# Product 2 of the third layer on the second Strassen level, its relation in three PE steps, and an order of issue with preferences of its own for that layer

## The chip, the core and the metric

The kernel runs on one core of a Trainium2 chip. The metric is device time in microseconds for one execution of the whole program, median of three runs. Profiles are of one execution each; the engines are called PE (matrix products), DVE, ACT and POOL (elementwise work) and SP (which issues most DMAs). One matmul in fp32 leaves two records in the trace.

## The reference

Four layers work on x of 128 graphs x 64 nodes x 512 features. Each normalises, applies relu, and adds a layer of attention over the graph's nodes to x. The third layer is the one that the change is about:

```python
h = jnp.maximum(_layernorm(x, axis=-1), 0.0)
x = x + _L2_gnn_ref(h, adj, L2_gnn_Wq, L2_gnn_Wk, L2_gnn_Wv)

def _L2_gnn_ref(neuron_states, adjacency, Wq, Wk, Wv):
    ...
    q = jnp.einsum('bnd,ed->bne', neuron_states, Wq)
    k = jnp.einsum('bnd,ed->bne', neuron_states, Wk)
    v = jnp.einsum('bnd,ed->bne', neuron_states, Wv)
    rel = jnp.einsum('bnd,bmd->bnm', q, k)
    rel = adjacency.T[None, :, :] * rel
    rel = rel / jnp.linalg.norm(rel, axis=2, keepdims=True)
    return jnp.einsum('bnm,bmd->bnd', rel, v)
```

The other three are attention with a softmax in 8 heads; the second and the fourth have an output projection, and the fourth a second normalisation behind it.

## The kernel before, in words

**Tiles.** The 8192 rows of x are cut into 16 tiles of 512 rows, and the main loop runs over n = 0 to 63: four layers of 16 tiles. Tile n is prepared (`layer_norm`, line 810) while tile n-1 is in its products. Its normalised rows are turned: ACT splits them into halves of words (`z`), SP issues a transposing DMA (`hp<-z`), and ACT copies `hp` into `hT` (`turn`, line 799). POOL then forms sums of quarters of hT (`sums_x`, line 855, tiles S and S2).

**Products on two levels.** Each projection of 512x512 by 512x512 is a Strassen product in Winograd's form: 7 products (1 to 7) of 256x256 by 256x256 instead of 8. One such product is 4 matmuls of 256 moving columns (`prod_T`, `prod_N`). A product may again be split into 7, of 128x128 by 128x128: then it is 7 matmuls of 128 columns (`prod_2`, line 905). The table LEVEL2 says which products of which projection are split: 4, 2 and 3 in most, but only 4 and 3 in `a2` and `v2`, the two projections of the third layer (`a2` has Wq and Wk folded into one matrix). Its sums of weights are made once (`sums_q_w`, line 705), its sums of x for each tile (`sums_q`, line 874). ORDERS (line 920 on) gives the order of the products in a projection: the digits in quotes are split, "a", "b" and "c" are the parts that the split products have in common, and each opens or shares a PSUM bank (HOME). ACT copies the first result of a quarter out of PSUM, DVE adds the later ones, POOL adds some pieces in SBUF (`projection`, line 928).

**The relation** of the third layer (`relate`, line 1331) is one step of PE for two tiles: for the tile before, the squares' sums (`ones` by `sq`) and rel by v into four banks; for the present tile, hT by gT into a fifth. DVE and ACT then make rel and its squares, POOL the reciprocal norms, and DVE scales the products of rel and v and adds them to xo, which SP stores. xo has one buffer, so its next load comes behind the store.

**The order of issue** is not that of the code. Every instruction is recorded as a step with its engine, a cost and its dependences (class Plan, line 57), and `order` (line 170) lists all of them engine by engine before anything is issued: of the steps that are ready on an engine it takes the earliest, and of those that with the smallest rank. The rank is a due time counted back from PE's sequence, plus an entry of the table PREFER for the step's kind (`kind`, line 160: engine, operation, tiles, size), less HASTE for steps that read PSUM. A PE step that opens a bank waits until one is free by that account, and may be at most WINDOW openings ahead. Accumulating DMAs of POOL (`add_out`, line 1292) add whole tiles to x in DRAM. All instructions are issued at line 313, which is why most profile lines name it.

Of the kernel before, what the change touches and what calls it, by code (L numbers as in the profile page):

```python
# [19 lines left out]
P = 128  # L20
G = 64
D = 512
# [34 lines left out]
class Plan:  # L57
# [4 lines left out]
    def __init__(self, nc):  # L62
        self.nc = nc
        self.steps, self.products, self.lags, self.front = [], [], {}, set()
        self.wrote, self.readers, self.known = {}, {}, {}
        self.group = None
        self.hot = set()
        for e in ("tensor", "vector", "scalar", "gpsimd", "sync"):
            setattr(self, e, Engine(self, e))
# [48 lines left out]
    def add(self, eng, calls, reads, writes, busy, late):  # L118
# [16 lines left out]
        self.steps.append([eng, calls, deps, busy, late])  # L135

# [23 lines left out]
    def kind(self, i):  # L160

        eng, calls = self.steps[i][:2]
        op, a, k = calls[0]
        aps = [v for v in list(a) + list(k.values()) if isinstance(v, bass.AP)]
        tags = [re.sub(r"(_\d+)+$", "", v.tensor.name) for v in aps]
        ins = [t for t in tags[1:] if t != "ident"][:1]
        name = f"{eng[:3]} {op} {tags[0]}<-{''.join(ins)}"
        return name if eng == "sync" or "x1" in name else f"{name} {aps[0].free_size()}"
# [170 lines left out]
class Pool:  # L339
# [34 lines left out]
ROOM = 5  # L374
ON_DVE = ""
WINDOW = 6
RESERVE = 0
HASTE = 17721.0
# [5 lines left out]
    "gps dma_start out_0_dram<-xo 2048": 5763,  # L384
    "gps dma_start x1<-kT": -946,
    "gps dma_start x1<-row": 14864,
    "gps memset mhalf<- 8": 5987,
    "gps memset ones<- 1": -3681,
    "gps tensor_scalar nb<-mv 4": -2896,
    "gps tensor_scalar ve<-mv 4": -6369,  # L390
    "gps tensor_tensor S2<-S 128": 9,
    "gps tensor_tensor S2<-S2 128": 741,
    "gps tensor_tensor S2<-hT 128": 632,
    "gps tensor_tensor S<-S 128": -41337,
    "gps tensor_tensor S<-S 512": -723,
    "gps tensor_tensor S<-hT 512": -6132,
    "gps tensor_tensor SO2<-SO 128": 396,
    "gps tensor_tensor SO2<-oT 128": -23951,
    "gps tensor_tensor SO<-SO 128": -50741,
    "gps tensor_tensor SO<-SO 512": 9602,  # L400
    "gps tensor_tensor SO<-oT 512": -33296,
    "gps tensor_tensor hT<-hT 128": -4880,
    "gps tensor_tensor kT<-kT 128": -5077,
    "gps tensor_tensor kT<-kT 256": 2384,
    "gps tensor_tensor kT<-kT 512": 11213,
    "gps tensor_tensor nb<-nb 1": -15986,
    "gps tensor_tensor nb<-nb 4": -3108,
    "gps tensor_tensor oT<-oT 128": -4027,
    "gps tensor_tensor qT<-qT 128": 12457,
    "gps tensor_tensor qT<-qT 256": -1197,  # L410
    "gps tensor_tensor rn<-ss 8": -6949,
    "gps tensor_tensor row<-hT 128": 11559,
    "gps tensor_tensor row<-row 128": -12998,
    "gps tensor_tensor rs<-ve 1": 813,
    "gps tensor_tensor rs<-ve 4": 10508,
    "gps tensor_tensor s<-hT 128": -31894,
    "gps tensor_tensor s<-s 1024": -44252,
    "gps tensor_tensor s<-s 128": 2292,
    "gps tensor_tensor v<-v 128": -5381,
    "gps tensor_tensor v<-v 256": -116,  # L420
    "gps tensor_tensor w<-w 128": 27797,
    "gps tensor_tensor w<-w 256": 34174,
    "gps tensor_tensor w<-w 512": 19861,
    "gps tensor_tensor xo<-xo 128": -2823,
    "gps tensor_tensor xo<-xo 256": 11906,
    "gps tensor_tensor xo<-xo 512": -26610,
    "sca activation kT<-mm 128": -14518,
    "sca activation kT<-mm 256": -7008,
    "sca activation qT<-mm 128": -14547,
    "sca activation qT<-mm 256": 1806,  # L430
    "sca activation s<-s 1024": 228608,
    "sca activation s<-s 256": 22995,
    "sca activation xin<-xin 512": 14211,
    "sca copy hT<-hp 1024": -86946,
    "sca copy hT<-mm 512": 16570,
    "sca copy kT<-mm 128": -51749,
    "sca copy kT<-mm 256": -10379,
    "sca copy kT<-mm 512": 312,
    "sca copy oT<-mm 512": 2819,
    "sca copy p5<-mm 128": -15649,  # L440
    "sca copy qT<-mm 128": -2476,
    "sca copy qT<-mm 256": -51590,
    "sca copy qT<-mm 512": -10049,
    "sca copy s<-hp 1024": 2630,
    "sca copy s<-mm 512": -22036,
    "sca copy v<-mm 128": -984,
    "sca copy v<-mm 256": 13038,
    "sca copy v<-mm 512": 40409,
    "sca copy w<-mm 128": 218,
    "sca copy w<-mm 256": 121,  # L450
    "sca copy xo<-mm 128": -10549,
    "sca copy xo<-mm 256": -34241,
    "sca copy xo<-mm 512": 7433,
    "sca copy z<-hp 1024": 3064,
    "sca copy z<-mm 512": -3311,
    "sca copy z<-oT 1024": -50937,
    "sca copy z<-s 1024": -9197,
    "sca copy z<-xin 1024": 18596,
    "syn dma_start a2d<-z": -1267,
    "syn dma_start adj2<-in_adj_dram": 25859,  # L460
    "syn dma_start bk1<-in_L1_gnn_bk_dram": 15719,
    "syn dma_start bq0<-in_L0_gnn_bq_dram": 5813,
    "syn dma_start bq1<-in_L1_gnn_bq_dram": -1214,
    "syn dma_start oT<-in_L2_gnn_Wq_dram": 3993,
    "syn dma_start oT<-in_L2_gnn_Wv_dram": 21834,
    "syn dma_start out_0_dram<-qT": -4023,
    "syn dma_start out_0_dram<-xo": -5129,
    "syn dma_start qT<-out_0_dram": -7867,
    "syn dma_start row<-in_L0_gnn_bv_dram": 12123,
    "syn dma_start row<-in_L3_gnn_b_proj_dram": -11681,  # L470
    "syn dma_start row<-in_L3_gnn_ln_beta_dram": -563,
    "syn dma_start row<-in_L3_gnn_ln_gamma_dram": 188,
    "syn dma_start v2d<-z": -4221,
    "syn dma_start w<-a2d": 3351,
    "syn dma_start w<-in_L0_gnn_Wk_dram": -18017,
    "syn dma_start w<-in_L0_gnn_Wq_dram": 6737,
    "syn dma_start w<-in_L0_gnn_Wv_dram": 12382,
    "syn dma_start w<-in_L1_gnn_Wk_dram": -32703,
    "syn dma_start w<-in_L1_gnn_Wo_dram": 24621,
    "syn dma_start w<-in_L1_gnn_Wq_dram": -15904,  # L480
    "syn dma_start w<-in_L1_gnn_Wv_dram": -8884,
    "syn dma_start w<-in_L3_gnn_w_proj_dram": 13379,
    "syn dma_start w<-in_L3_gnn_w_qkv_dram": -1695,
    "syn dma_start w<-v2d": -8508,
    "syn dma_start x1<-xo": -647,
    "syn dma_start xin<-in_x_dram": -8353,
    "syn dma_start xin<-x1": -13444,
    "syn dma_start xo<-in_x_dram": 31957,
    "syn dma_start xo<-x1": 15761,
    "ten matmul mm<-S 128": 4706,  # L490
    "ten matmul mm<-S 256": 5870,
    "ten matmul mm<-SO 128": -29146,
    "ten matmul mm<-SO 256": 3875,
    "ten matmul mm<-hT 128": 7283,
    "ten matmul mm<-hT 256": -141,
    "ten matmul mm<-hT 64": -4249,
    "ten matmul mm<-oT 128": -1749,
    "ten matmul mm<-oT 256": -7085,
    "ten matmul mm<-qT 64": 9858,
    "ten matmul mm<-row 128": -14789,  # L500
    "ten matmul mm<-s 1": -12970,
    "ten matmul mm<-s 128": 4783,
    "ten matmul mm<-s 64": -16805,
    "ten matmul mm<-w 128": -1692,
    "ten transpose mm<- 128": 4281,
    "ten transpose mm<-s 128": -23333,
    "ten transpose mm<-xin 128": -1673,
    "vec bn_aggr mv<-st 2": -11581,
    "vec bn_stats st<-kT 6": -1271,
    "vec bn_stats st<-w 6": 63642,  # L510
    "vec bn_stats st<-xin 6": 100131,
    "vec reciprocal sr<-sr 16": -17544,
    "vec scalar_tensor_tensor qT<-z 512": -2888,
    "vec scalar_tensor_tensor xo<-z 512": -15061,
    "vec scalar_tensor_tensor z<-kT 512": 159895,
    "vec scalar_tensor_tensor z<-w 512": -3755,
    "vec tensor_copy hT<-mm 512": 11299,
    "vec tensor_copy ss<-mm 4": 198,
    "vec tensor_reduce mx<-s 16": -348,
    "vec tensor_reduce sr<-s 16": -429,  # L520
    "vec tensor_scalar mask0<-adj2 64": -11809,
    "vec tensor_scalar mask1<-mask1 64": 5681,
    "vec tensor_scalar mask3<-adj2 64": 232,
    "vec tensor_tensor S<-S 512": -23945,
    "vec tensor_tensor kT<-mm 256": 16733,
    "vec tensor_tensor kT<-mm 512": -27839,
    "vec tensor_tensor oT<-mm 512": -20089,
    "vec tensor_tensor p5<-mm 128": -246,
    "vec tensor_tensor qT<-mm 128": 4915,
    "vec tensor_tensor qT<-mm 256": -3702,  # L530
    "vec tensor_tensor qT<-mm 512": 16865,
# [59 lines left out]
def gnn_stack_kernel(  # L591
# [83 lines left out]
    def finer(name, n):  # L675
        return LEVEL2.get(name, "") if n >= FIRST or name[1] != "0" else ""
# [936 lines left out]
```

## Time and profile before

| | |
|---|---|
| median of 3 runs | 2765.62 us (2763.9 to 2766.32) |
| the profiled execution, its own time | 2762.89 us |
| its span, first to last instruction | 2760.9 us |
| granted PE clock, mean | 0.998 |
| instructions | 71834, of which 29259 matmul records |
| HBM read and written | 120.63 MB, 102.76 MB |

The rows of the profile's groups name line, engine, operation, `out<-in` with the form, then the count, the total busy time and the mean of one, and the idle time of the engine just before with what ended it. In a timeline a row gives the start, the length, the engine, the operation and how many are merged in it. Consecutive matmuls overlap in the records, so the distance of two starts, and not the length of one, says what a matmul costs in a dense stretch. The third layer lies between about 1500 and 1945 us of the span.

### The profile page before, as it was taken

The numbers are of one execution on the slowest core, as the hardware profiler recorded it, in microseconds if no ns is written. First come the engines' busy times: TensorE is split into PE (matmuls) and PEld (weight loads), VectorE is DVE, ScalarE is ACT, GpSimd is POOL, SyncE is SP. The second block draws the span as 40 slices with busy tenths as digits, with TensorE's granted clock in tenths as the row PEclk, the third lists the DMA queues.
The fourth block names the chain that finished last, engine by engine and source line by source line (L and its number), as shares of the span: only waits on it lengthen the run. The fifth ranks groups of instructions, "written<-read, shape, count | busy, mean of one in ns | idle before, by whom it ended". The sixth has DMA issues, their size and how long they took to land.

```text
span 2760.9 us, 71834 instructions
## 1 busy us (share of the span) xinstructions
PE 2740.6 (99%) x29259; PEld 2508.3 (91%) x29259; DVE 1718.2 (62%) x3298; ACT 1897.4 (69%) x3141; POOL 2062.3 (75%) x2823
## 2 busy tenths in 40 slices
PE   9999999999999999999999999999999999999998
PEld 8999899999999999999989898989999999999997
DVE  6666566665656556556555555545577677677777
ACT  6788688888776766767756666565766666666662
POOL 5667768779978778688689654546887887887885
PEclk9999999999999999999999999999999999999999
DMA  5666576666365556565575756567544563654644
GB/s 142 158 145 133 145 158 142 154 143 168 76 125 111 96 110 114 94 112 103 108 142 106 181 154 165 153 153 177 116 89 81 113 118 78 122 109 81 127 92 97
DMA packets 635018, 344.47 MB, mean 125 GB/s; under 512 B 484288, under 2 KB 565952, under 8 KB 634688
## 3 DMA queue, kind: packets, MB, share of 16 engines
q1 hardware_dynamic: 601424, 273.83, 43.2%
q0 software_dynamic: 33264, 66.06, 14.6%
q8 instruction: 229, 3.75, 0.5%
q14 instruction: 101, 0.83, 0.1%
HBM read 120.63 MB, written 102.76 MB: 81 GB/s over the span
## 4 chain that ended last, share of the span: by engine, by line
PE 88%; POOL 5%; ACT 2%; DMA 2%; issue 1%; DVE 1%; SPq 0%; POOLq 0%; ACTq 0%; DVEq 0%
PE mm L313 88%; POOL w L313 1%; POOL s L313 1%; DMA hp<-z 1%; POOL S L313 1%; POOL SO L313 1%; ACT z L313 0%; SPq L313 0%; DMA xin<-in_x_dram 0%; ACT s L313 0%; ACT xin L313 0%; DMA xo<-x 0%; POOL v L313 0%; ACT qT L313 0%; POOL xo L313 0%
## 5 line engine op out<-in xcount | busy, mean ns | idle before, releaser
L313 PE MATMUL mm<-S,w 128*128 128x256 f32 (+1 forms) x4600 | 912.9, 337 | 0.9 <-ACT kT L313 0.8
L313 PEld LDWEIGHTS mm<-S,w 128*128 128x128 f32 x4600 | 743.4, 191 | 62.0 <-ACT kT L313 1.3
L313 PE MATMUL mm<-hT,w 128*128 128x128 f32 (+1 forms) x3392 | 606.9, 311 | 1.3 <-ACT p L313 0.9
L313 PEld LDWEIGHTS mm<-hT,w 128*128 128x128 f32 x3392 | 517.8, 191 | 46.6 <-ACT qT L313 4.3
L313 PE MATMUL mm<-w,S 128*128 128x128 f32 (+1 forms) x2604 | 523.2, 338 | 4.5 <-ACT v L313 3.6
L313 PEld LDWEIGHTS mm<-w,S 128*128 128x128 f32 x2604 | 430.0, 191 | 42.8 <-ACT v L313 4.2
L313 DVE TENSOR_TENSOR v<-mm,v 128x512 f32<-128x512 f32 (+2 forms) x440 | 255.9, 589 | 255.7 <-PE mm L313 149.9
L313 DVE TENSOR_TENSOR qT<-mm,qT 128x512 f32<-128x512 f32 (+2 forms) x440 | 255.8, 592 | 237.2 <-PE mm L313 173.0
L313 DVE TENSOR_TENSOR kT<-mm,kT 128x256 f32<-128x256 f32 (+1 forms) x433 | 258.0, 612 | 233.2 <-PE mm L313 124.1
L313 ACT COPY v<-mm 128x128 f32<-128x128 f32 (+1 forms) x380 | 172.7, 456 | 285.9 <-PE mm L313 275.4
L313 ACT COPY hT<-hp 128x1024 uint16<-128x1024 uint16 x252 | 338.5, 1363 | 31.6 <-DMA hp<-z 31.0
L313 PE MATMUL mm<-w,hT 128*128 128x128 f32 (+1 forms) x1872 | 345.0, 313 | 0.1
L313 PEld LDWEIGHTS mm<-w,hT 128*128 128x128 f32 x1872 | 287.5, 191 | 19.2
L313 POOL TENSOR_TENSOR S<-hT 128x512 f32<-128x512 f32 (+1 forms) x172 | 201.7, 1267 | 108.8 <-ACT hT L313 108.8
L313 PE MATMUL mm<-w,SO 128*128 128x256 f32 (+1 forms) x1302 | 263.5, 335 | 0.1
L313 ACT COPY z<-xin 128x1024 uint16<-128x1024 uint16 x252 | 260.0, 1081 | 0.0
L313 POOL TENSOR_TENSOR qT<-qT,p 128x128 f32<-128x128 f32 (+1 forms) x170 | 111.9, 670 | 189.1 <-DVE qT L313 123.0
L313 ACT COPY s<-hp 128x1024 uint16<-128x1024 uint16 x188 | 251.7, 1370 | 0.1
L313 POOL TENSOR_TENSOR s<-s,mx 128x1024 f32<-128x1024 f32 x96 | 210.6, 2237 | 45.1 <-DVE mx L313 45.1
L313 PEld LDWEIGHTS mm<-w,SO 128*128 128x128 f32 x1302 | 212.2, 191 | 19.5 <-DVE kT L313 2.7
L313 ACT COPY z<-s 128x1024 uint16<-128x1024 uint16 x188 | 190.2, 1048 | 34.3 <-POOL s L313 34.0
L313 ACT ACTIVATE xin<-xin,nb,rs 128x512 f32<-128x512 f32 x256 | 200.5, 827 | 13.6 <-POOL nb L313 13.6
(117 smaller groups left out, 4605.1 us busy)
## 6 DMA issues: line engine op xcount, KB each, us to landing
xin<-x SPq DMA_DIRECT2D x128, 256.0 KB, 3.5
xin<-in_x_dram SPq DMA_DIRECT2D x64, 256.0 KB, 4.0
x<-row POOLq DMA_DIRECT2D x16, 1024.0 KB, 13.8
xin<-out_dram SPq DMA_DIRECT2D x64, 256.0 KB, 3.7
out_dram<-row POOLq DMA_DIRECT2D x16, 1024.0 KB, 14.1
x<-xo POOLq DMA_DIRECT2D x15, 1024.0 KB, 9.4
out_dram<-xo POOLq DMA_DIRECT2D x15, 1024.0 KB, 10.2
xo<-in_x_dram SPq DMA_DIRECT2D x32, 256.0 KB, 4.1
```

Of the source, the lines that this page charges most:

```text
L313: getattr(getattr(self.nc, eng), op)(*a, **k)
```

## The change

1. From the third tile of the third layer on (n >= 2*NB + 2, 14 tiles), both projections split product 2 too (DEEP = "423"). The weights' sums for it are made behind the second tile (`deepen`). The sums of x get eight more places in a buffer that is free in that layer (tag "oT"). The code for products 7 and 5 comes along, with its room, but DEEP does not name them.
2. `relate` makes three steps of PE: sums of squares together with hT by gT, and one for each half of rel by v; so two or three banks are opened at a time instead of five.
3. The kinds of the table PREFER get a suffix " 2" for steps of the third layer (`phase`), the whole table has new values, and HASTE goes from 17721 to 24970.

```diff
@@ Plan.add
         self.steps.append([eng, calls, deps, busy, late])
+        self.phases.append(self.phase)
@@ Plan.kind
-        return name if eng == "sync" or "x1" in name else f"{name} {aps[0].free_size()}"
+        size = "" if eng == "sync" or "x1" in name else f" {aps[0].free_size()}"
+        return name + size + (self.phases[i] if hasattr(self, "phases") else "")
@@ constants
+DEEP = "423"
...
-HASTE = 17721.0
+HASTE = 24970.0
 PREFER = {
...
-    "ten matmul mm<-S 256": 5870,
+    "ten matmul mm<-S 256": 6187,
+    "ten matmul mm<-S 256 2": -3891,
...
+    "ten matmul mm<-s 256 2": 9177,
...
-    "syn dma_start xo<-x1": 15761,
+    "syn dma_start xo<-x1 2": 13243,
...
@@ finer, deepen
     def finer(name, n):
+        if name[1] == "2" and n >= 2 * NB + 2:
+            return DEEP
         return LEVEL2.get(name, "") if n >= FIRST or name[1] != "0" else ""
...
+    def deepen(name, at):
+        if "rooms" not in W2:
+            W2["rooms"] = p1.tile([P, KC * KC, P], F32, tag="SO", name="rooms")
+        for i, q in enumerate("75"):
+            W2[name][q] = W2["rooms"][:, at + 3 * i : at + 3 * i + 3]
+        for q in DEEP:
+            if q not in LEVEL2[name]:
+                sums_q_w(name, q, gps.tensor_tensor)
@@ relate
-        plan.end(580)
+        plan.end(290 if old else 0)
+        if old:
+            pos = []
+            for g in range(2):
+                po = quads(f"pv_{m}_{g}", "qf", q=2)
+                pos.append(po)
+                plan.begin()
+                for p in range(2):
+                    for b, y in QUARTERS:
+                        j = b ^ y
+                        pe.matmul(
+                            po[j][half(y), p, :], old[1][half(b), 2 * g + p, :],
+                            v[half(b), 2 * g + p, j * H2 : (j + 1) * H2], start=True, stop=True,
+                        )
+                plan.end(385)
@@ sums_of
             fine = [fine[:, i] for i in range(4)]
+            if n >= 2 * NB + 2:
+                more = p1.tile([P, KC * KC, P], F32, tag="oT", name=f"more_{n}")
+                fine += [more[:, 8 * (n % 2) + i] for i in range(8)]
@@ main loop
+        plan.phase = " 2" if l == 2 else ""
...
             run(projection(prod_T, "a2", xop, f"g_{n}", gT))
+            if k == 1:
+                deepen("a2", 0)
...
             run(projection(prod_N, "v2", xop, f"v_{n}", v))
+            if k == 1:
+                deepen("v2", 6)
```

In the third layer the order of a projection's products so goes from (1, 5, 6, a, 2, b, 7, c, "4", "3") to (1, 5, 6, a, 7, b, "2", c, "4", "3").

## The prediction

> **What bounds the kernel now.** I read the page first, its busy times and its chain:
>
> ```profile
> PE 2740.6 (99%) x29259; PEld 2508.3 (91%) x29259; DVE 1718.2 (62%) x3298; ACT 1897.4 (69%) x3141; POOL 2062.3 (75%) x2823
> ...
> PE 88%; POOL 5%; ACT 2%; DMA 2%; issue 1%; DVE 1%; SPq 0%; POOLq 0%; ACTq 0%; DVEq 0%
> ```
>
> PE is busy for all but 20.3 us of the 2760.9 and carries 88% of the chain. So a saving counts if it shortens PE's own stream, or removes one of its few waits. Next I asked for busy time by stretch of time; the first figure behind the stretch is its length, the second PE's busy time, then PEld, DVE, ACT, POOL:
>
> ```profile
> 180.00:230.00 50.00, 49.40 (x551) 45.68 (x549) 30.16 (x55) 42.35 (x73) 38.12 (x50) 1.00 0.57 126
> 350.00:360.00 10.00, 9.25 (x59) 8.33 (x58) 3.13 (x7) 10.00 (x19) 2.11 (x4) 1.00 0.49 107
> 660.00:760.00 100.00, 99.14 (x1084) 91.03 (x1083) 59.22 (x111) 81.33 (x136) 98.42 (x144) 1.00 0.46 94
> 1430.00:1445.00 15.00, 11.41 (x59) 9.82 (x58) 4.53 (x8) 6.40 (x10) 10.98 (x16) 0.90 1.19 204
> 1530.00:1540.00 10.00, 9.12 (x53) 8.16 (x52) 5.02 (x14) 2.73 (x7) 9.23 (x15) 1.00 0.96 222
> 1578.60:1859.90 281.30, 281.30 (x2498) 253.32 (x2494) 145.00 (x361) 173.15 (x270) 143.44 (x210) 1.00 0.60 153
> 2725.00:2740.00 15.00, 12.71 (x205) 11.71 (x204) 13.51 (x27) 6.53 (x15) 7.60 (x8) 1.00 0.01 2
> ```
>
> The sixth row is ten tiles of the third layer, 28.13 us each: PE never idles there, while DVE, ACT and POOL are free for 48%, 38% and 49%. The other rows are the places where PE does wait. Then the timeline of PE in that layer, for the price of one matmul of each width:
>
> ```profile
> 1707.12 0.83 PE L313 MATMUL mm<-w,S 128*128 128x128 f32 x6
> 1707.79 1.89 PE L313 MATMUL mm<-hT,w 128*128 128x256 f32 x8
> 1709.52 0.39 PE L313 MATMUL mm<-s,w 128*128 128x128 f32 x2
> ```
>
> The records overlap, so the price is the distance of starts: 8 records of 256 columns take 1709.52 - 1707.79 = 1.73 us, 216 ns each; 6 records of 128 columns take 0.67 us, 112 ns each. Over the whole trace the medians are 216 and 111.5.
>
> **Product 2, 28 times.** From the third tile of the layer on, both projections take product 2 on the second level: 14 tiles x 2 = 28. The listing of both programs' PE queues has it so (224 records of 256 columns go, 392 of 128 come), which rules out that the change does not do what it says. One product was 4 matmuls = 8 records x 216 = 1728 ns and becomes 7 matmuls = 14 x 111.5 = 1561 ns, 167 ns less. 28 x 167 = **-4.7 us**, all on PE, which has no idle time there to swallow it.
>
> It adds beside PE: POOL +92 additions (56 sums of x, 28 of a result quarter, 8 of weights), 0.46 us each by the third layer's rows, so 6 x 0.46 = 2.8 us a tile against 13.8 us free; ACT +28 copies of 128x128 at 0.27, 0.5 us a tile against 10.8 free; DVE no more instructions, but in each of its 28 projections two additions grow from 128 to 256 columns and one from 256 to 512 (0.285, 0.417, 0.69 us), so +0.53 each, 1.1 us a tile against 13.6 free. I cost these at nothing. If the cover went, the four sums of x, which stand on POOL between ACT's copy into hT and the next tile's first matmuls, would be what PE waits for: 1.8 us a tile. The wider additions hold one PSUM bank 0.13 to 0.27 us longer.
>
> The Trainium skill ("TensorE: Matmul & The Clock Gate", Back-to-back issue gap) gives a sustained spacing of 81 ns at 128 columns and 131 at 512, so that narrow matmuls cost more per column. Interpolated to 98 ns at 256 (an estimate from that page), a product would go from 781 to 1134 ns, and 28 of them would add 9.9 us. This trace's 216 and 111.5 ns disagree, and they decide.
>
> **The relation in three steps.** It was one PE step that needed five banks free at once; its rows:
>
> ```profile
> 1518.44 1.89 PE L313 MATMUL mm<-w,S 128*128 128x256 f32 x8
> 1520.26 0.57 PE L313 MATMUL mm<-ones,s 64*64 64x1 f32 x14
> ...
> 1520.75 1.92 PE L313 MATMUL mm<-v,s 64*64 64x256 f32 x30
> 1522.60 2.08 PE L313 MATMUL mm<-qT,hT 128*64 128x64 f32 x64
> 1524.62 1.56 PE L313 MATMUL mm<-w,hT 128*128 128x256 f32 x6
> ```
>
> It takes 1524.62 - 1520.26 = 4.36 us, and entering it 0.09 (1.82 us for eight records). In the new listing the three steps stand next to each other in all 15 full tiles, as half of the v products, ones and qT, the other half: nothing is put between, so only the seams change. By starts of matmuls in the trace, the old seams were ones to v 46 ns, v to qT 312, qT to wide 158: 516. The new: v to ones, ones to qT, qT to v, v to wide. The last is seen once, 313. For v to ones I take the 84 of one v matmul to the next (46 to 107); for ones to qT the 155 of the one other crossing from 64x64 into qT (58, qT to qT, to 312); for qT to v the 158 of qT to wide (58 to 312). That is 710, with one v-to-v gap less (107 by the mean): 710 - 107 - 516 = 87 ns, 15 times, **+1.3 us**; with all low ends -148 ns, -2.2 us; with all high ends +421 ns, +6.3 us. The fewer banks at once save nothing in a stretch where PE never waits.
>
> The Trainium skill ("TensorEngine Tiling (Array Packing)", Key Properties) says that each change of tiling mode drains the engine; the order has four such changes a tile instead of three. That is the rule of a rival below; of the traces' crossings, 312 ns (v to qT) agrees and 155 and 158 do not show a full one.
>
> **The order everywhere else.** All preferences are new and those of the third layer are separate, so all queues move: SP, POOL, ACT and DVE alike. PE's waits that a new order can touch are the rows above without the fourth: 0.60 + 0.75 + 0.86 + 0.88 + 2.29 = 5.4 us. The one at 1530 to 1540 is DVE waiting for a load of xo; in the new SP listing the first load of xo, and so the store and the second load, stand ahead of four transposes and four loads of xin that it stood behind. At 2725 to 2740 the last tile's values wait for DVE. For the others I only know that the order differs. What I do not expect to go is the fourth row, the largest:
>
> ```profile
> 1423.51 4.53 SPq L313 DMA_TRANSPOSE hp<-z  x1
> ...
> 1425.17 1.28 POOL L313 DMA_DIRECT2D x<-row  x1
> ...
> 1436.21 1.89 PE L313 MATMUL mm<-w,S 128*128 128x256 f32 x8
> ...
> 1439.87 1.33 ACT L313 COPY hT<-hp 128x1024 uint16<-128x1024 uint16 x1 [5.17 <-DMA hp<-z]
> ```
>
> A transpose beside POOL's 1 MB accumulating transfers lands after 16.4 us (of 25 such waits the median is 4.3), ACT stands before its copy, the copy of v behind it comes late, and PE's eight records from 1436.21 last until 1441.69: 5.48 - 1.73 = 3.75 us. Then the granted clock is 0.50 from 1441.9 to 1445.2 (0.90 over the row's 15 us), and the next eight records take 1.73 us more: 5.5 in all. SP's listing there (transposes and loads of w) is unchanged, and so is the order of POOL's two transfers. I take half of the 5.4 us as the gain, **-2.7 us**; bounds -10.9 (all of it and the 5.5) and +5.5 (a second such stall).
>
> **The sum.** -4.7 + 1.3 - 2.7 = -6.1 us. The profiled execution took 2762.89 (2.0 around its span): 2756.8. The median of the runs, 2765.62, is 2.7 above it: **2759.5 us**, -0.22%. About 0.2% (5.5 us, 2760.1) is what a measurement of this kernel can tell from no change.
>
> **Rivals.** *Only the stream changes* (0.28): the new order takes elsewhere what it gives; -4.7 + 1.3 = -3.4, 2762.2. For it: 5.4 us of waits in 2760 is little to win, and each queue is new. *Seams drain* (0.06): every seam costs its high end, -4.7 + 6.3 - 2.7 = -1.1, 2764.5; against it the 155 and 158 ns. *The boundary stall goes too* (0.08): POOL's transfer comes 3 us later against the transpose; -6.1 - 5.5, 2754.0. *A stall like it at more places* (0.09, slower): transposes of hT now stand in SP's queue ahead of xin loads with POOL's two accumulating transfers before them swapped, x_14<-xo ahead of x_15<-row. The stall of before would have been none with a landing below 16.4 - 5.5 = 10.9 us; from there on each us is one of PE's. Two new ones give -3.4 + 11 = +7.6, 2773.2; one gives 2767.7. *Narrow matmuls cost more than the pitch* (0.03, slower): busy time by count in the groups, 353.9 us / 2304 = 154 ns and 634.9 / 2720 = 233, would make a product 2150 instead of 1867 ns; 28 x 0.283 = +7.9, with the rest +6.5, 2772.1. It turns to slower above 1728 / 14 = 123 ns; the starts say 111.5.
>
> **Chances.** Forecast 0.46, boundary stall gone 0.08: faster 0.54. Only the stream, seams: same 0.34. The two slower ones: 0.12. The range, 2753.5 to 2767.5, reaches from the boundary stall gone to one new stall, and takes in the seams' bounds; it leaves out two stalls, narrow matmuls and the outer ends.
>
> **What would show it.** The third layer's period between relations falls from 28.13 us by 0.33 - 0.09 to 27.89, and PE stays busy throughout; product 2 shows 14 records at 111.5 ns; the three relation steps together take 4.45 us; PE waits about 3.6 us again near 1437; 1530 to 1540 has no wait on DVE. Wrong would be: idle PE inside the third layer, a landing of a transpose over 10.9 us at a second place, or a period above 28.1.

## The result and the profile after

The changed kernel takes **2753.05 us** (median of 6 runs, 2752.1 to 2755.85), the kernel before 2766.49 in the same session: a ratio of 0.9954, 95% interval 0.9941 to 0.9967. It is faster, as forecast, but by about twice the forecast: 2759.5 was 6.4 us too high, and 2753.05 lies 0.45 us below the low end of the range. The profiled execution has a span of 2750.3 us, 10.6 less than before. By the medians the difference is 13.4 us: the profiled execution of the kernel before was 3.6 us quicker than that session's median, the changed kernel's 0.95 us. What follows explains the 10.6 us between the two profiles.

First the page of the changed kernel, its busy times and its chain:

```profile
PE 2734.5 (99%) x29427; PEld 2506.0 (91%) x29427; DVE 1735.3 (63%) x3298; ACT 1897.0 (69%) x3169; POOL 2102.2 (76%) x2915
...
PE 89%; POOL 6%; ACT 2%; DVE 1%; DMA 1%; issue 1%; SPq 0%; POOLq 0%; ACTq 0%; DVEq 0%
```

PE has 168 records more and 6.1 us less busy time; ACT has the 28 copies and POOL the 92 additions more. Busy time cannot say where 10.6 us went, so next three of the stretches of time that the prediction shows (length, then PE, PEld, DVE, ACT, POOL, the granted clock, DMA):

```profile
1430.00:1445.00 15.00, 15.00 (x203) 13.67 (x202) 6.69 (x10) 7.61 (x13) 15.00 (x21) 1.00 1.13 246
1530.00:1540.00 10.00, 10.00 (x65) 9.27 (x65) 3.69 (x8) 4.07 (x9) 9.83 (x19) 1.00 0.88 188
1571.40:1849.90 278.50, 278.50 (x2604) 250.63 (x2600) 156.57 (x360) 177.88 (x293) 170.77 (x270) 1.00 0.64 157
```

The first row is the surprise: PE is busy for all of the 15 us in which it had been busy for 11.41, and its clock stayed at 1.00. In the second PE no longer waits. The third is again ten tiles of the third layer, with no idle time.

How much came from where is read by matching: the same PE step is looked up in both traces, and the start after less the start before is followed along the program. In the third layer the mark is the first matmul of each relation, because the steps inside it have changed their order.

| stretch (time in the kernel before) | forecast | measured |
|---|---|---|
| start and layers 0 and 1, to 1390 | part of -2.7 | -2.2 |
| boundary before the third layer, 1390 to 1483 | 0 | **-4.4** |
| first tiles of the third layer, 1483 to 1520 | 0 | +0.2 |
| 15 periods between relations, 1520 to 1941 | -3.4, and part of -2.7 | -3.4 |
| change to the fourth layer, 1941 to 1986 | 0 | +0.45 |
| fourth layer, 1986 to 2699 | 0 | **-2.3** |
| tail, from 2699 | part of -2.7 | +1.0 |
| sum | -6.1 | -10.6 |

**The boundary.** Rows of SP, POOL, ACT and PE there, in order of time:

```profile
1421.27 4.24 SPq L316 DMA_TRANSPOSE hp<-z  x1
1422.53 1.27 POOL L316 TENSOR_TENSOR w<-w 128x512 f32<-128x512 f32 x1
1426.19 5.58 SPq L316 DMA_TRANSPOSE hp<-z  x2
1427.93 1.53 POOL L316 TENSOR_TENSOR w<-w 128x128 f32<-128x128 f32 x3 [4.12 <-DMA w<-a2d]
1429.39 1.29 POOL L316 DMA_DIRECT2D x<-row  x1
1432.31 1.34 ACT L316 COPY hT<-hp 128x1024 uint16<-128x1024 uint16 x1
1433.93 3.62 PE L316 MATMUL mm<-w,S 128*128 128x256 f32 x16
```

POOL's transfer `x<-row` was issued 1.66 us after the first transpose in the kernel before; here 1429.39 - 1421.27 = 8.12 us after it. Four additions of weights now stand between `row<-hT` and it in POOL's queue, and they wait 4.12 us for a load. The transpose lands after 8.7 us instead of 16.3, and PE runs its 16 records without a break.

The three additions of 128 columns are the change's own: they begin the sums of weights that product 2 needs on the second level. In the code `deepen` stands behind the second tile of the third layer, but these three need only one loaded block of a2, and the order of issue puts them here, before the layer begins. The profile has 120 such additions, the one before 112. All six kernels whose product 2 is split have three of them here, the four others none.

**The relation** in the steady tiles, PE alone:

```profile
1709.74 1.09 PE L316 MATMUL mm<-v,s 64*64 64x256 f32 x16
1710.66 0.58 PE L316 MATMUL mm<-ones,s 64*64 64x1 f32 x16
1711.17 2.08 PE L316 MATMUL mm<-qT,hT 128*64 128x64 f32 x64
1713.18 1.09 PE L316 MATMUL mm<-v,s 64*64 64x256 f32 x16
1714.21 1.99 PE L316 MATMUL mm<-w,S 128*128 128x256 f32 x8
```

From the first start to that of the columns behind it: 1714.21 - 1709.74 = 4.47 us, by the median of the steady tiles 4.461 against 4.356. The period between relations, by starts, goes from 28.07 to 27.85 us.

**The fourth layer.** Nothing of its work is changed. The view of waits shows none of PE's there that explains 2.3 us. The waits of the weight loads (PEld) do, between 2040 and 2700 us: total, times, longest. First the kernel before, then the changed one:

```profile
PEld mm L313 <- ACT qT L313: 3.0, 11, 0.3
PEld mm L313 <- DVE kT L313: 2.7, 12, 0.5
PEld mm L313 <- issue: 0.3, 1, 0.3
```

```profile
PEld mm L316 <- issue: 1.7, 3, 1.1
PEld mm L316 <- ACT v L316: 0.4, 1, 0.4
```

A weight load normally runs beside the matmul ahead of it. Where it starts late here, the matmul records behind it start late too, by 105 ns for each such wait in the mean, which no wait of PE shows. 24 such waits became 4; 20 x 0.105 = 2.1 us of the 2.3. Four more kernels with the new order (experiments 2, 4, 7 and 8) gain 1.8 to 2.2 us in this stretch; two with the old order (experiments 1 and 3) gain nothing.

### The profile page after: what moved, and what is told of

It reads as the page before. It is cut to its first block, busy times and chain, and to the rows that moved or that the text cites. A ratio compares the mean times of both kernels' runs of the same rounds, so it can differ in the third digit from the quotient of the medians.

```text
span 2750.3 us, 72249 instructions
## 1 busy us (share of the span) xinstructions
PE 2734.5 (99%) x29427; PEld 2506.0 (91%) x29427; DVE 1735.3 (63%) x3298; ACT 1897.0 (69%) x3169; POOL 2102.2 (76%) x2915
## 4 chain that ended last, share of the span: by engine, by line
PE 89%; POOL 6%; ACT 2%; DVE 1%; DMA 1%; issue 1%; SPq 0%; POOLq 0%; ACTq 0%; DVEq 0%
PE mm L316 89%; POOL w L316 2%; POOL s L316 1%; POOL S L316 1%; DMA hp<-z 1%; POOL SO L316 0%; ACT z L316 0%; ACT s L316 0%; DMA x<-xo 0%; ACT xin L316 0%; POOL xo L316 0%; ACT kT L316 0%; DVE st L316 0%; DVE sr L316 0%; POOL v L316 0%
## 5 line engine op out<-in xcount | busy, mean ns | idle before, releaser
L316 PE MATMUL mm<-S,w 128*128 128x256 f32 (+1 forms) x4516 | 900.1, 338 | 1.6 <-issue 1.0
L316 PEld LDWEIGHTS mm<-S,w 128*128 128x128 f32 x4516 | 734.5, 191 | 62.5 <-POOL S L316 1.0
L316 PE MATMUL mm<-hT,w 128*128 128x128 f32 (+1 forms) x3364 | 593.3, 307 | 0.8 <-ACT p L316 0.7
L316 PE MATMUL mm<-w,S 128*128 128x256 f32 (+1 forms) x2520 | 514.9, 340 | 0.0
L316 PEld LDWEIGHTS mm<-w,S 128*128 128x128 f32 x2520 | 418.8, 191 | 42.0 <-ACT s L316 3.1
L316 DVE TENSOR_TENSOR qT<-mm,qT 128x512 f32<-128x512 f32 (+2 forms) x440 | 264.6, 609 | 196.7 <-PE mm L316 149.3
L316 PE MATMUL mm<-w,hT 128*128 128x128 f32 (+1 forms) x1844 | 326.7, 307 | 1.1 <-DVE p L316 0.7
L316 PEld LDWEIGHTS mm<-w,hT 128*128 128x128 f32 x1844 | 277.8, 191 | 19.4 <-ACT s L316 0.9
L316 POOL TENSOR_TENSOR qT<-qT,p 128x256 f32<-128x256 f32 (+1 forms) x184 | 118.0, 651 | 185.4 <-DVE qT L316 105.4
L316 PE MATMUL mm<-w,oT 128*128 128x128 f32 (+1 forms) x1252 | 222.3, 303 | 0.2 <-ACT oT L316 0.2
```

Of the source, the lines that this page charges most:

```text
L316: getattr(getattr(self.nc, eng), op)(*a, **k)
```

## The experiments

Times are medians; ratios are to the kernel before in the same session. "Landing" is from the issue of the first transpose at the boundary to its end.

**1. The transfer moved in the kernel before.** Only the place of one DMA in POOL's queue changes:

```diff
 POOL: row<-hT
-POOL: DMA x<-row
 POOL: SO<-oT
 POOL: SO<-oT
+POOL: DMA x<-row
```

> The kernel before, with one instruction moved: POOL's accumulating transfer x_14<-row stands behind the two additions SO<-oT that followed it. Theory: the 16.4 us landing of the transpose at 1423.5 us, PE's wait of 3.59 us behind it and the granted clock of 0.50 for 3.4 us after that come from this transfer being issued 1.7 us behind the transpose. Then the span falls by 5.5 us to about 2755.4 (at least by 4), the transpose lands within 10.9 us and the clock stays at 1.00 near 1440 us. Rival: the loads of w issued around the transposes delay them, which are the same here: the span stays at 2760.9 within 1 us and PE waits 3.6 us.

Measured: 2757.92 us, ratio 0.9973 (0.9962 to 0.9983). The span of its profile, 2758.2, came out neither way; but that execution had lost 1.9 us in its first 20 us and 0.8 more by 1390, and from there to 1483 it gained 5.1 us, as expected. Rows at the boundary:

```profile
1425.59 4.93 SPq L321 DMA_TRANSPOSE hp<-z  x1
...
1435.78 1.27 POOL L321 DMA_DIRECT2D x<-row  x1
...
1437.31 1.35 ACT L321 COPY hT<-hp 128x1024 uint16<-128x1024 uint16 x1
...
1438.93 2.32 PE L321 MATMUL mm<-w,S 128*128 128x256 f32 x10
```

The transfer comes 10.2 us after the transpose, the landing is 9.4 us, PE does not stand and the clock stays up. One DMA's place in one queue is worth 5 us in the profile, and 7.4 us by the medians of the runs (4.7 to 10.5 by the interval).

**2. The transfer moved back in the changed kernel**, ahead of the four additions of weights:

```diff
 POOL: row<-hT
+POOL: DMA x<-row
 POOL: w<-w 512, w<-w 128 (three)
-POOL: DMA x<-row
```

> The changed kernel, with one instruction moved the other way: POOL's transfer x_14<-row stands ahead of the four sums of weights (w 512 columns, three of 128) whose wait of 4.12 us for the load of w delays it to 1429.4 us. Theory: the transfer is then issued within 2 us of the transpose at 1421.3 us, which lands after 14 us or more, PE waits over 3 us, the granted clock falls to 0.50 for 3.4 us, and the span rises by 4.4 to 5.5 us to 2754.7 to 2755.8. Rival: the stall went for another reason of the new order: the span stays at 2750.3 within 1 us.

Measured: 2755.41 us, ratio 0.9962 (0.9949 to 0.9976), span 2750.8. The mechanism came back, the price did not:

```profile
1421.61 4.47 SPq L324 DMA_TRANSPOSE hp<-z  x1
1423.39 1.29 POOL L324 DMA_DIRECT2D x<-row  x1
...
1434.67 1.89 PE L324 MATMUL mm<-w,S 128*128 128x256 f32 x8
1436.83 1.34 ACT L324 COPY hT<-hp 128x1024 uint16<-128x1024 uint16 x1 [3.68 <-DMA hp<-z]
1438.04 0.57 ACT L324 COPY v<-mm 128x512 f32<-128x512 f32 x1
1438.66 1.56 PE L324 MATMUL mm<-w,S 128*128 128x256 f32 x6 [2.11 <-ACT v L324]
```

The transfer is 1.78 us behind the transpose, the landing 15.2 us, and PE's next records start 1438.66 - 1434.67 - 1.73 = 2.26 us late. No half clock follows. Against the changed kernel only 1.2 us are lost by 1483, because that one has small waits of PE from 1445 on (0.75 us for DVE at 1450.99) that this order lacks; at the end of the span 0.5 us is left. By the runs it may be more: the ratios, 0.9962 here and 0.9954 for the changed kernel, are 2.2 us apart, but their intervals overlap, and the profiled execution was the quickest of five. So the late landing and a stall are shown to come back, a price in the whole time is not.

Six orders at this place, with experiments 3 and 4:

| kernel | x<-row after the transpose | landing | PE stands | clock after it |
|---|---|---|---|---|
| before | 1.66 us | 16.3 | 3.75 | 0.50 for 3.413 us |
| order alone | 2.86 | 18.1 | 5.17 | 0.50 for 3.413 us |
| changed, transfer back | 1.78 | 15.2 | 2.26 | 1.00 |
| split alone | 7.50 | 10.1 | 0 | 1.00 |
| changed | 8.12 | 8.7 | 0 | 1.00 |
| before, transfer later | 10.19 | 9.4 | 0 | 1.00 |

PE starts 1.82 us after the landing at the earliest, and runs out of work 14.4 us (before) or 14.8 us (second and third row) after the transpose's issue. So it stands for the landing less 12.6 or 13.0 us: 3.7, 5.1 and 2.2, as measured. The kernels of the other experiments fit in: with the transfer 1.92 us after the transpose (experiment 5) the landing is 16.7 us, with 6.3 to 8.1 us (experiments 6 to 8) it is 8.7 to 10.2.

**3. The split alone**: product 2 split as in the change, with the old preferences and the relation in one step.

```diff
+DEEP = "423"
...
+        if name[1] == "2" and n >= 2 * NB + 2:
+            return DEEP
...
+            if k == 1:
+                deepen("a2", 0)
...
+            if k == 1:
+                deepen("v2", 6)
```

> Product 2 of the third layer on the second level alone: the relation in one step, and preferences and HASTE as before, none for the third layer. Theory that the parts add up: 28 x 167 ns less PE, period of the third layer's tiles 28.13 - 0.33 = 27.80 us, everything else as before: span 2756.2. Rival, that an order fits only the work it was made for: the new steps are put where the old preferences leave them, PE waits in the third layer, where it did not wait at all, for banks or for POOL's and DVE's additions, the period stays above 28.0 us and the span does not fall below 2760.

Measured: 2765.53 us, ratio 0.9999 (0.9990 to 1.0008). The waits of PE from 1480 to 1950:

```profile
PE mm L316 <- ACT v L316: 2.8, 5, 1.4
PE mm L316 <- POOL S L316: 1.8, 2, 1.4
PE mm L316 <- ACT qT L316: 1.0, 1, 1.0
PE mm L316 <- DVE mv L316: 0.6, 1, 0.6
```

The boundary no longer stalls. The shortest periods are 27.83 us, 0.24 below 28.07 where the columns alone were to give 0.33: two records of 128 columns in each of these tiles start late, 213 and 144 ns behind the one before instead of 111.5. Above all the 6.2 us of waits, most of them in the first seven tiles (periods up to 32.9 us), take the gain back: from 1483 to 1945 this kernel loses 6.3 us.

**4. The order alone**: the new preferences, product 2 unsplit, the relation in one step.

```diff
-HASTE = 17721.0
+HASTE = 24970.0
...
+        plan.phase = " 2" if l == 2 else ""
```

> The new preferences and HASTE alone, with their own for the third layer: product 2 unsplit and the relation in one step, as before. Theory that the parts add up: without the split's and the relation's -3.3 us the span is 2750.3 + 3.3 = 2753.6, with the third layer's period at 28.13, no stall at the boundary, and the fourth layer's period 0.21 us shorter than before (51.05 to 50.84), as in the changed kernel. Rival: the new preferences for the third layer fit only its split work: PE waits there, the period is above 28.3 us and the span at or above 2757; the fourth layer's period, whose work is the same, is 0.21 us shorter in both theories.

Measured: 2765.13 us, ratio 0.9997 (0.9988 to 1.0006), span 2764.6: 11 us over the theory that the parts add up. As the rival says, PE waits in the third layer, 4.1 us in a few tiles; but most periods are 28.07 us as before. The boundary stall is larger (PE 5.17 us); the weight loads of the fourth layer wait twice instead of 24 times, and from 1986 to 2699 it gains 1.8 us. So the gain in the fourth layer belongs to the order; that at the boundary does not: without the split, the three additions of weights are not there.

**5. The relation alone**, in three steps, in the kernel before.

```diff
-        plan.end(580)
+        plan.end(290 if old else 0)
+        if old:
+            pos = []
+            for g in range(2):
...
+                plan.end(385)
```

> The kernel before with the relation in three steps and nothing else; product 2 unsplit, the old preferences. Theory 1 (cost of the seams alone): relation 4.46 instead of 4.36 us, 15 times 0.106 is 1.6 us more, span about 2762.5 us, and the wait of PE of 3.6 us before the third layer stays. Theory 2 (an order fits one set of steps only, and the old preferences no longer fit): new PE waits of more than 3 us in all, span 2766 us or more.

Measured: 2799.24 us, ratio 1.0125 (1.0111 to 1.0140). Both theories hold, in different layers. In the third the period is 28.18 us in all of the first 14, + 0.106, and the boundary stall is there. In the fourth, which the edit does not touch, PE waits, in the view of waits from 2050 to 2700:

```profile
PE mm L313 <- DVE kT L313: 21.1, 39, 1.2
```

These are three waits in each of 13 tiles. Of the 33.8 us that this kernel loses from 1986 to 2699, they are 21.1. Behind them in three tiles (at 2163, 2218 and 2699 us) the granted clock is 0.50 for 3.413 us:

```profile
2160.23 0.46 PE L313 MATMUL mm<-kT,qT 64*64 64x64 f32 x16 [0.24 <-DVE kT L313]
2161.04 0.93 PE L313 MATMUL mm<-kT,qT 64*64 64x64 f32 x48 [0.35 <-DVE kT L313]
2162.97 1.83 PE L313 MATMUL mm<-kT,qT 64*64 64x64 f32 x64 [1.00 <-DVE kT L313]
```

**6. The changed kernel with the relation in one step.**

```diff
-        plan.end(290 if old else 0)
+        plan.end(580)
```

> The changed kernel with the relation as one step of PE again, as it was before; product 2 is split and the new preferences hold. Theory 1 (the three steps are only a cost, 106 ns more in each tile by the traces): 15 times 0.106 is 1.6 us less, span about 2748.7 us, third layer without PE waits. Theory 2 (the three steps are what lets the new order fit: one step takes four more banks at once and gives the other engines nothing to do in between, as in the runs of the split alone and of the order alone, which lost 6 to 8 us in the third layer): PE waits of several us between 1480 and 1950 us, span 2757 us or more.

Measured: 2800.24 us, ratio 1.0129 (1.0115 to 1.0144). Theory 2, and far more than it said: the span is 48.5 us longer than the changed kernel's. The largest waits of PE from 1480 to 1950 (21.7 us with the smaller ones), then those from 2050 to 2700:

```profile
PE mm L316 <- ACT v L316: 11.5, 12, 1.4
PE mm L316 <- DVE v L316: 2.8, 3, 1.5
```

```profile
PE mm L316 <- ACT kT L316: 11.2, 13, 1.1
```

The second view is of a layer without a relation. The granted clock is 0.50 for 6.827 us from 1534 on, behind waits of 1.26 and 0.99 us. So the reason that I gave, banks taken at once and nothing done in between, is not shown: it would cost in the third layer alone, and the changed kernel itself issues the three steps without a break. What the two runs have in common is an order made from preferences that were fitted to another list of steps.

**7 and 8. The relation's steps in other orders**, the other queues as in the changed kernel, in 15 tiles:

```diff
 PE: v half
-PE: ones, qT
 PE: v half
+PE: ones, qT
```

> The changed kernel with one thing moved: in the 15 tiles of the third layer, the step of PE with the columns of ones and the relation's own products is issued behind both halves of the product with v, not between them; all else is in the order of the changed kernel. Theory (the relation pays once for every change of tile shape, as the records of the changed kernel give it: from 256-wide columns into v 309 ns, v to ones 196, ones to qT 123, qT to v 152, v back to the columns 306, sum 1086 ns; in the new order 309, v to v 7, v to ones 196, ones to qT 123, qT to the columns 152 as in the kernel before, sum 787): 0.30 us less in each tile, so the period between relations goes from 27.89 to about 27.6 us and the span from 2750.3 to about 2745.8 us. Rival (the second half's banks or the hT copy are not free yet, or DVE, which needs the ones and the relation, gets them 1 us later and makes PE wait behind): PE waits appear at the relation in most tiles, the period stays at 27.9 us or grows, span 2750 or above.

```diff
-PE: v half
 PE: ones, qT
+PE: v half
 PE: v half
```

> The changed kernel with the first half of the product with v issued behind the step with ones and the relation's own products, so that both halves are last. By the same list of seams: into ones 309 ns, ones to qT 123, qT to v 152, v to v 7, v to the columns 306, sum 897 against 1086: 0.19 us less in each tile, period about 27.7 us, span about 2747.5 us. Rival: as for the other order, waits of PE take it back, period 27.9 us or more and span 2750 us or above. If the seams depended on the number of changes alone (three instead of four inside the relation in both orders), both orders would gain the same.

Measured: 2754.92 us, ratio 0.9968 (0.9957 to 0.9979), span 2751.4; and 2757.54 us, ratio 0.9975 (0.9966 to 0.9983), span 2755.8. My list of seams fails. Medians of the steps' lengths, in the steady tiles:

| order | first | second | third | sum |
|---|---|---|---|---|
| changed: v; ones, qT; v | 0.914 | 2.523 | 1.024 | 4.461 |
| v, v; ones, qT | 0.914 | 0.863 | 2.523 | 4.300 |
| ones, qT; v, v | 2.575 | 0.914 | 0.973 | 4.462 |

The distance from one record to the next at a seam holds the v matmul's own run, so it does not go away with the seam. What does is read from the table: 51 ns each time that the array enters 64x64 tiles from another shape, 110 ns when v is followed by the columns, and nothing between v and ones. That gives 0.161 and 0 us; I had said 0.30 and 0.19.

I also miscounted the third order: it has four changes of tile shape (into ones, ones to qT, qT to v, v to the columns), as the changed kernel has, and only the second has three. By that count the sums agree, 4.461 and 4.462 against 4.300.

The 0.161 us did not come through either: the period is 27.83, only 0.02 shorter. Two steps with 128 columns grew from 0.893 to 0.941 and from 0.667 to 0.757. Ahead of the second stands a weight load that waits, in nine tiles from 1550 to 1930 us; the changed kernel has no such wait there:

```profile
PEld mm L327 <- ACT qT L327: 2.0, 9, 0.2
```

The third order also waits in its third to sixth period (28.6, 29.2, 29.1, 28.0 us), which is 3.4 of the 5.5 us by which its span is longer. Neither beats the changed kernel.

## Why the prediction came out as it did

- **Columns, -4.7 us.** Right in the changed kernel: 28.07 - 0.334 + 0.106 = 27.84, measured 27.85; in a steady tile the 28 added records of 128 columns take 3.13 us and the 16 that went took 3.46. PE stayed busy there. That the price holds in another order is not shown: with the split alone it was 0.24 a tile, and 6.2 us of waits besides. (The forecast's 28.13 to 27.89 was a window by ten with its edges; by starts it fell by 0.222 where 0.24 was said.) The page's 81 and 131 ns a matmul (the Trainium skill, "TensorE: Matmul & The Clock Gate", Back-to-back issue gap), by which the columns would have cost 9.9 us more, do not hold for these records.
- **Relation, +1.3 us.** 106 ns where 87 was forecast: +1.6. The sum was near by luck, its parts were not: I had v to ones at 84 ns and ones to qT at 155, the records say 196 and 123, and experiments 7 and 8 show that such distances cannot be taken apart and put together anew.
- **Order elsewhere, -2.7 us.** Mis-sized. At the places I named it gave 1.7 us, where I had taken 2.7: -2.2 in layers 0 and 1, -0.5 in the period with 1530 to 1540, where DVE no longer makes PE wait, and +1.0 in the tail, which has new waits just ahead of 2694 and 2702. The -2.2 is hardly clear of the spread between executions: at 1390 us the four profiles with the old order of these layers differ by 4.1 us (experiments 1, 3 and 5 stand at +2.7, -1.4 and +0.4 against the kernel before), and the six with the new order lie between -2.2 and -1.1. What I had not looked for was the waits of the weight loads in the fourth layer, 2.3 us, because I read only PE's waits. The two changes of layer around the third gave 0.7 back.
- **The step that failed** is "What I do not expect to go is the fourth row". SP's listing is unchanged there, and so is the order of POOL's two transfers, as I said; I did not look at what stands between them. Four additions of weights and their wait for a load delay the second by 6.5 us. Three of the four are among the "8 of weights" that I had counted beside PE and costed at nothing: I looked for their price on PE, and not for what they delay on POOL. So the largest gain, 4.4 us, is a by-product of the split that nothing in the change aimed at. I had its outcome as a rival, "POOL's transfer comes 3 us later against the transpose", at 0.08 and 2754.0 us: it is the case that came true. Experiments 1 and 2 show the place of the transfer as the cause of the late landing, in both directions; the time followed in full only in the first, because in the second PE stood for 2.26 us and the clock stayed up. My threshold for the landing, 10.9 us, was too low: I took the whole 5.5 us from 16.4, though 1.7 of it is clock that is lost only once PE has stood; 12.6 to 13.0 is measured.
- **What stays open.** Why a transpose lands late when the transfer follows it closely: the experiments show that it does, not by what. The 105 ns of a late weight load are read from the traces and from the order alone; no experiment took away one such wait by itself. Experiments 5 and 6 lose 34 to 35 us against the kernel before, most of it in waits of PE and some in the half clock behind them; the rest is not accounted for. Why the planner's order brings these waits, also in a layer that the edit does not touch, the runs do not say.

## What to carry to other kernels

When a scheduler reorders everything, compare each queue's full listing around the largest stall, not only the two instructions that meet there; and look at the weight loads' waits as well as the matmuls'. An order that is fitted to one list of steps has no price by parts: the split alone and the order alone were each worth nothing, the relation alone cost 34 us, and together they gave 13. Test a stall's cause by moving one instruction in one queue, in both directions.

## What the runs showed of the hardware

- A transposing DMA that was issued 1.7 to 2.9 us ahead of POOL's 1 MB accumulating transfer landed after 15.2 to 18.1 us, in three kernels; with 7.5 to 10.2 us between them it landed after 8.7 to 10.1 us, in three others. The four other kernels fall into the same two groups (1.9 us: 16.7; 6.3 to 8.1 us: 8.7 to 10.2).
- PE standing for 3.75 and 5.17 us was followed by a granted clock of 0.50 for 3.413 us, which cost the next eight records 1.73 and 1.67 us; 2.26 us were followed by no half clock. The Trainium skill ("TensorE: Matmul & The Clock Gate", Part 1: The HAM clock gate) puts the half clock behind one idle window of 3413 ns. The three stalls agree with that, the profile of experiment 5 does not: there PE was still busy for 1.82 of the 3.41 us ahead of 2163.2 us, in which its longest wait was 1.00 us, and the clock fell to 0.50 for 3.413 us all the same. It did so behind the same three waits in three of 13 tiles.
- A step with v took 51 ns more when the array came to its 64x64 tiles from another shape, and 110 ns more when the 128x128 columns followed it. From v to ones, which are both 64x64, the distance of two starts is 196 ns, as between two groups of v. From the last qT (128x64) to the next start it is 151 or 152 ns, whether v or the columns follow, where 52 is usual between groups of qT. The Trainium skill ("TensorEngine Tiling (Array Packing)", Key Properties) says that a change of mode drains the engine; these distances agree, with a price at each of these changes of shape and none where it stays.
